# The softmax maximum of a stretch of context: an all-reduce on GpSimd in place of transposes and a product with a diagonal

## The chip, the cores and the metric

The kernel runs on one core of one Trainium2 chip. The metric is the device time of one execution, in microseconds (us). Engines are named as in the profile: PE (TensorE, PEld for its weight loads), DVE (VectorE), ACT (ScalarE), POOL (GpSimd), SP (SyncE, which issues the DMAs here).

## What is computed

One layer of a perceiver: cross attention between 256 latent tokens and a context of 25088 rows, then self attention, then a mixture of experts, everything in float32 with 512 features. The change lies in the cross attention, from latents to context:

```
h = layernorm(x)                                   # x: 256 x 512
Q = h @ Wq_c.T + bq_c;  K = ctx @ Wk_s.T + bk_s;  V = ctx @ Wv_s.T + bv_s
char2sub = softmax(Q @ K.T / sqrt(512)) @ V        # over 25088 context rows
sub2char = (context queries over the latents, interpolated back to 256)
gate = sigmoid(concat(char2sub, sub2char) @ Wg.T + bg)
x = x + gate * char2sub + (1 - gate) * sub2char
x = x + self_attention(layernorm(x))
x = x + shared_ffn(layernorm(x)) + routed_expert_ffn(layernorm(x))   # 32 experts, one per token
```

## The kernel before

The keys' weights are folded into the queries ahead of the loop (`aT`, and `cq` for the part that comes from the keys' bias), and the values' weights are applied behind it. In the loop a score is therefore `ctxT` times `aT`, and the output `o_sb` collects the probabilities times raw context rows. A score tile has context rows on its 128 partitions and the 256 latent tokens along its columns, so the softmax's maximum of a token is a maximum over partitions.

The context comes in 49 blocks of 512 rows. A stretch is three blocks (`SPAN`), so there are 16 full stretches and a last one of one block, 17 in all. For each stretch:

- `score` runs 48 matmuls of 128x256 (L392) into PSUM banks of the pool `ps_mm`, which has four. ACT copies each pair to `st` (L396), and DVE keeps a running maximum `mx` (L398, L400, L401). The columns' last maximum, L401, leaves one 128x256 tile.
- `maxima` turns `mx` into the running maximum per token, in two forms. As a column per token (`m_new`, tokens on partitions): two transposes on PE (L409) and a reduce on DVE (L411), `cq` added, maximum with the old one. `alpha` is the factor by which the old output shrinks. As a row of tokens on all partitions (`mbc`): `m_new` less `cq` scales an identity (`dg`, L428), a matmul with ones spreads it over partitions (L430), and ACT copies it out of PSUM (L432).
- `exponentials` subtracts `mbc` from each pair of `st` on DVE (L440), takes the exponential on ACT (L443) and adds the pairs up on POOL (L445, L447) into `ls`, then into `l_acc` with the factor `al` (L452 to L456).
- `width_sums` (`diffs`, L484 to L487) and `token_sums` (`sums`, L496 to L499) prepare on DVE the operands of `products`: a fast multiplication scheme with seven matmuls of 128x256 (L519) for each half block, 42 in a stretch.
- `collect` adds the four banks to `o_sb` on DVE. Its row `u2` shares one buffer (the tag "row", one buffer) with `dg` and `al`.

The program's order puts the stretches one inside the other: while PE runs `score(s + 1)`, DVE works on `token_sums(s)` and two blocks of `width_sums`. Then PE runs `products(s)`, while DVE, ACT and POOL do `maxima(s + 1)` and `exponentials(s + 1)`, and DVE the third block's `width_sums`. The framework schedules instructions on each engine within this order; each engine works its queue in order. Before the loop, scores and maxima of stretch 0 have no products beside them. Behind the loop, `weigh_last` handles the last block, and a matmul with ones sums `l_acc` over partitions (L572).

Of the kernel before, what the change touches and what calls it, by code (L numbers as in the profile page):

```python
# [2 lines left out]

# [7 lines left out]
F32 = mybir.dt.float32  # L11
I32 = mybir.dt.int32
AF = mybir.ActivationFunctionType
ALU = mybir.AluOpType
AX = mybir.AxisListType

P = 128
H = 512
KC = H // P
N = 256  # L20
NT = N // P
# [27 lines left out]
def perceiver_layer(  # L49
# [23 lines left out]
    nc = tc.nc  # L73
# [5 lines left out]
    small = ctx.enter_context(tc.tile_pool(name="small", bufs=4))  # L79
# [4 lines left out]
    def mm_bank(name):  # L84
        return ps_mm.tile([P, 512], F32, tag="mm", name=name)
# [4 lines left out]
    def tr_bank(name):  # L90
        return ps_tr.tile([P, 512], F32, tag="tr", name=name)
# [54 lines left out]
    ident = cpool.tile([P, P], F32, tag="ident", name="ident")  # L146
    make_identity(nc, ident)
    ones = cpool.tile([P, P], F32, tag="ones", name="ones")
# [107 lines left out]
    cq = first_half.tile([P, NT], F32, tag="cq", name="cq")  # L256

    with tc.tile_pool(name="pro", bufs=1) as pro:
# [18 lines left out]
        for t in range(NT):  # L277
            pm = mm_bank(f"cq_{t}")
            for c in range(KC):
                nc.tensor.matmul(  # L280
                    pm[:, 0:1], qT[:, c, ts(t, P)], bias_col("bk_s", c),
                    start=(c == 0), stop=(c == KC - 1),
# [22 lines left out]
        for n in (0, NT, 1, NT + 1):  # L305
            pm = mm_bank(f"s2_{n}")
            for c in range(KC):
                nc.tensor.matmul(
                    pm[:, :N], selT[:, c, ts(n, P)], bT[:, c, :],
                    start=(c == 0), stop=(c == KC - 1),  # L310
                )
            nc.vector.tensor_tensor(p2[:, n, :], pm[:, :N], bk, ALU.add)
            mx = small.tile([P, 1], F32, tag="s2_mx", name=f"s2_mx{n}")
# [17 lines left out]
        for t in range(NT):  # L331
            pm = mm_bank(f"vc_{t}")
            for c in range(KC):
                nc.tensor.matmul(
                    pm, xnT[:, c, ts(t, P)], wv_c_sb[:, c, :],
                    start=(c == 0), stop=(c == KC - 1),
                )
            evacuate(vc[:, t, :], pm)
        for k in range(NT):
            pt = tr_bank(f"p2T_{k}")  # L340
# [3 lines left out]
        for o in range(KC):  # L344
            pm = mm_bank(f"s2c_{o}")
            for k in range(NT):
                nc.tensor.matmul(
                    pm[:, :N], vc[:, k, ts(o, P)], p2T[:, k, :],
                    start=(k == 0), stop=(k == NT - 1),
# [27 lines left out]
    with tc.tile_pool(name="crows", bufs=3) as crows, tc.tile_pool(name="cwork", bufs=2) as cw:  # L377
        state = {"m": None, "mbc": None}

        def score(s):  # L380
            tiles = range(firsts[s], min(firsts[s] + SPAN, NBLK))
            n_pairs = 2 * len(tiles)
            st = cw.tile([P, 2 * SPAN, 2 * N], F32, tag="st", name=f"st_{s}")
            mx = cw.tile([P, 2 * N], F32, tag="rows", name=f"mx_{s}", bufs=1)
            for i in range(n_pairs):
                b, h = tiles[i // 2], i % 2
                if h == 0 and b + 2 < NBLK:
                    load_cols(b + 2)
                pm = mm_bank(f"sc_{s}_{i}")
                for u in range(2):  # L390
                    for c in range(KC):
                        nc.tensor.matmul(  # L392
                            pm[:, ts(u, N)], cols[b][:, c, ts(2 * h + u, P)], aT[:, c, :],
                            start=(c == 0), stop=(c == KC - 1),
                        )
                nc.scalar.copy(st[:, i, :], pm)  # L396
                if i == 1:
                    nc.vector.tensor_tensor(mx, st[:, 0, :], st[:, 1, :], ALU.max)  # L398
                elif i > 1:
                    nc.vector.tensor_tensor(mx, mx, st[:, i, :], ALU.max)  # L400
            nc.vector.tensor_tensor(mx[:, :N], mx[:, :N], mx[:, N:], ALU.max)  # L401
            return st, mx

        def maxima(s, mx):


            pt = mm_bank(f"mxT_{s}")
            for t in range(NT):
                nc.tensor.transpose(pt[:, ts(t, P)], mx[:, ts(t, P)], ident)  # L409
            m_new = small.tile([P, NT], F32, tag="m", name=f"m_{s}")  # L410
            nc.vector.tensor_reduce(  # L411
                m_new, pt[:, :N].rearrange("p (t q) -> p t q", t=NT), AX.X, ALU.max
            )
            nc.vector.tensor_tensor(m_new, m_new, cq, ALU.add)
            alpha = ones
            if s > 0:
                nc.vector.tensor_tensor(m_new, m_new, state["m"], ALU.max)
                dm = small.tile([P, NT], F32, tag="dm", name=f"dm_{s}")
                nc.vector.tensor_tensor(dm, state["m"], m_new, ALU.subtract)
                alpha = small.tile([P, NT], F32, tag="alpha", name=f"alpha_{s}")  # L420
                nc.scalar.activation(alpha, dm, AF.Exp, scale=xscale)
            state["m"] = m_new

            mc = small.tile([P, NT], F32, tag="mc", name=f"mc_{s}")
            nc.vector.tensor_tensor(mc, m_new, cq, ALU.subtract)
            dg = cw.tile([P, N], F32, tag="row", name=f"dg_{s}", bufs=1)
            for t in range(NT):
                nc.vector.tensor_scalar(dg[:, ts(t, P)], ident, mc[:, t : t + 1], None, ALU.mult)  # L428
            pb = mm_bank(f"mbc_{s}")
            nc.tensor.matmul(pb[:, :N], ones, dg, start=True, stop=True)  # L430
            mbc = cw.tile([P, 1, N], F32, tag="mbc", name=f"mbc_{s}")
            nc.scalar.copy(mbc[:, 0, :], pb[:, :N])  # L432
            return mbc, alpha

        def exponentials(s, st, mbc):
# [118 lines left out]
        nc.gpsimd.memset(o_sb, 0.0)  # L554
        st, mx = score(0)
        mbc, alpha = maxima(0, mx)
        exponentials(0, st, mbc)
        for b in range(3):
            load_rows(b)
        for s in range(len(firsts) - 1):  # L560
            st_next, mx = score(s + 1)
            a, sums = token_sums(s, st)
            ready = {b: width_sums(b) for b in range(firsts[s], firsts[s] + 2)}
            mbc, alpha_next = maxima(s + 1, mx)
            bank = products(s, a, sums, ready)
            exponentials(s + 1, st_next, mbc)
            collect(s, bank, alpha)
            st, alpha = st_next, alpha_next
# [10 lines left out]
    with tc.tile_pool(name="mix", bufs=1) as mp:  # L579
        oT = mp.tile([P, KC, N], F32, tag="oT", name="oT")  # L580
        for t in range(NT):
            pt = tr_bank(f"oT_{t}")
# [9 lines left out]
        for o in range(KC):  # L592
            for c in range(KC):
                nc.tensor.matmul(
                    gates[o][:, :N], wg_sb[:, KC + c, ts(o, P)], s2cT[:, c, :],
                    start=(c == 0), stop=False,
# [3 lines left out]
        for o in range(KC):  # L600
            pm = acc_bank(f"c2sT_{o}")
            for c in range(KC):
                nc.tensor.matmul(
                    pm[:, :N], wv_s_sb[:, c, ts(o, P)], oT[:, c, :],
                    start=(c == 0), stop=(c == KC - 1),
# [8 lines left out]
        for o in range(KC):  # L614
            pm = gates[o]
            for c in range(KC):
                nc.tensor.matmul(
                    pm[:, :N], wg_sb[:, c, ts(o, P)], c2sT[:, c, :],
                    start=False, stop=(c == KC - 1),
# [21 lines left out]
    with tc.tile_pool(name="att", bufs=1, reuse_waits="tile") as at:  # L641
        h1T = at.tile([P, KC, N], F32, tag="h1T", name="h1T")
        vh = at.tile([P, NT, HD], F32, tag="vh", name="vh")
        with tc.tile_pool(name="att1", bufs=1, reuse_waits="tile") as at1:
            h1 = at1.tile([P, NT, H], F32, tag="h1", name="h1")
            for t in range(NT):
                normalize(h1[:, t, :], x_sb[:, t, :], st1[:, t], f"ln1_{t}")
                pt = tr_bank(f"h1T_{t}")
# [139 lines left out]
    for t in range(NT):  # L788
# [3 lines left out]
        pt = tr_bank(f"h2T_{t}")  # L792
# [3 lines left out]
    mx = fp.tile([P, NT], F32, tag="mx", name="mx")  # L796
    for t in range(NT):
        pm = tr_bank(f"lg_{t}")
        for c in range(KC):
            nc.tensor.matmul(  # L800
                pm[:, :E], h2T[:, c, ts(t, P)], gw_sb[:, c, :],
                start=(c == 0), stop=(c == KC - 1),
# [318 lines left out]
```

## Time and profile before

| | us |
|---|---|
| median of three runs | 1304.01 (1302.05 to 1304.39) |
| profiled execution, its own time | 1304.49 |
| its span, first to last instruction | 1302.8 |
| PE busy, the whole span | 1161.5 (89%) |
| POOL busy, the whole span | 177.9 (14%) |
| cross attention over the context | about 60 to 723 |

Times in the profile count from the span's start. A row of the order of time gives start, length, engine, line, operation, output and inputs, and in square brackets how long the engine had been idle and what it waited for. A float32 matmul of 128x256 shows as two records. "L392" is line 392 of the kernel before; in the changed kernel, lines behind the change are five less. Behind the cross attention come self attention and the expert stage, whose chain is mostly DMA of expert weights.

### The profile page before, as it was taken

How to read it: one execution, taken by the hardware profiler on the slowest of the kernel's cores; microseconds unless marked ns; L12 is line 12 of the kernel's file. 1: busy time of each engine (PE TensorE's matmuls, PEld its weight loads, DVE VectorE, ACT ScalarE, POOL GpSimd, SP SyncE). 2: the span in 40 equal slices, each digit the busy share in tenths (PEclk: the TensorE clock that was granted, in tenths of full speed). 3: DMA queues.
4: the chain of work that ended last, by engine and by line, in shares of the span. 5: the costliest groups of instructions: out<-in, count | busy, mean ns of one | idle time of the engine just before them, and what ended most of it. 6: DMA issues, size and time to landing. Idle time of an engine off the chain costs nothing.

```text
span 1302.8 us, 16384 instructions
## 1 busy us (share of the span) xinstructions
PE 1161.5 (89%) x6796; PEld 842.8 (65%) x6796; DVE 617.4 (47%) x1079; ACT 227.3 (17%) x473; POOL 177.9 (14%) x149
## 2 busy tenths in 40 slices
PE   7989999999999999999999999898898677667665
PEld 6778888888888888888888656554544232222221
DVE  2257778877778777788776435511101010000000
ACT  0222212222212222122221223311000000000000
POOL 1023113332123331133322000000000000000000
PEclk9989999999999999999999999899999998988898
DMA  9544444444434454444431390599999999999995
GB/s 388 218 159 176 148 157 162 162 162 161 162 138 160 159 177 147 158 162 162 161 130 65 113 403 2 194 378 429 430 429 428 431 429 430 429 430 430 429 431 230
DMA packets 30892, 330.43 MB, mean 254 GB/s; under 512 B 3552, under 2 KB 3680, under 8 KB 4064
## 3 DMA queue, kind: packets, MB, share of 16 engines
q1 hardware_dynamic: 30816, 329.36, 63.6%
q8 instruction: 55, 0.90, 0.3%
q14 instruction: 21, 0.17, 0.0%
HBM read 328.82 MB, written 0.52 MB: 253 GB/s over the span
## 4 chain that ended last, share of the span: by engine, by line
PE 68%; DMA 27%; DVE 3%; issue 1%; ACT 1%; SPq 0%; DVEq 0%; ACTq 0%
PE sc L392 25%; PE p L519 21%; DMA rd<-in_ro_d_dram 9%; DMA rg<-in_ro_g_dram 9%; DMA ru<-in_ro_u_dram 8%; PE d L923 1%; PE ru L904 1%; PE rg L904 1%; PE acc L932 1%; PE y L750 1%; PE vh L659 1%; PE q L681 1%; PE k L681 1%; PE mbc L430 1%; PE shg L942 1%; PE qT L221 1%
## 5 line engine op out<-in xcount | busy, mean ns | idle before, releaser
L392 PE MATMUL sc<-aT,ctxT 128*128 128x256 f32 x1568 | 343.5, 381 | 0.6 <-DMA ctxT<-in_cxT_dram 0.6
L392 PEld LDWEIGHTS sc<-aT,ctxT 128*128 128x128 f32 x1568 | 299.4, 191 | 42.2 <-issue 1.0
L519 PE MATMUL p<-diffs,sums 128*128 128x256 f32 x576 | 155.8, 379 | 0.0
L519 PEld LDWEIGHTS p<-diffs,sums 128*128 128x128 f32 x576 | 109.4, 190 | 14.9
L923 PE MATMUL d<-rd,actT 128*32 128x512 f32 x512 | 75.5, 712 | 39.3 <-DMA rd<-in_ro_d_dram 31.0
L904 PE MATMUL ru<-ru,xg 128*32 128x256 f32 x1024 | 69.8, 415 | 41.4 <-DMA ru<-in_ro_u_dram 41.4
L396 ACT COPY st<-sc 128x512 f32<-128x512 f32 x98 | 57.4, 586 | 280.7 <-PE sc L392 280.7
L447 POOL TENSOR_TENSOR ls<-ls,st 128x512 f32<-128x512 f32 x64 | 97.1, 1517 | 33.8 <-ACT st L443 30.0
L400 DVE TENSOR_TENSOR mx<-mx,st 128x512 f32<-128x512 f32 x64 | 44.2, 691 | 116.1 <-ACT st L396 116.1
L519 PE MATMUL p<-ctx,st 128*128 128x256 f32 x384 | 98.5, 379 | 0.0
L930 DVE TENSOR_SCALAR selT<-keys,slot_key 128x256 f32<-128x256 f32 x32 | 11.2, 353 | 179.1 <-PE acc L932 179.1
L910 DVE TENSOR_TENSOR act<-act,ru 128x256 f32<-128x256 f32 x32 | 13.5, 422 | 167.8 <-PE ru L904 160.3
L445 POOL TENSOR_TENSOR ls<-st 128x512 f32<-128x512 f32 x17 | 25.1, 1476 | 493.8 <-ACT st L443 493.8
L904 PEld LDWEIGHTS ru<-ru,xg 128*32 128x32 f32 x1024 | 33.4, 119 | 75.1 <-DMA ru<-in_ro_u_dram 50.0
L932 PE MATMUL acc<-d,selT 128*128 128x512 f32 x128 | 66.3, 643 | 16.5 <-ACT d L101 16.5
L519 PEld LDWEIGHTS p<-ctx,st 128*128 128x128 f32 x384 | 72.9, 190 | 9.9
L443 ACT ACTIVATE st<-st 128x512 f32<-128x512 f32 x98 | 60.8, 630 | 100.2 <-DVE st L440 99.5
L440 DVE TENSOR_TENSOR st<-st,mbc 128x512 f32<-128x512 f32 x98 | 66.2, 718 | 21.8 <-ACT mbc L432 21.8
L484 DVE TENSOR_TENSOR diffs<-ctx 128x512 f32<-128x512 f32 x48 | 64.0, 1334 | 9.1 <-DMA ctx<-in_cx_dram 9.1
L904 PE MATMUL rg<-rg,xg 128*32 128x256 f32 x1024 | 63.9, 382 | 0.9 <-DVE xg L99 0.2
L923 PEld LDWEIGHTS d<-rd,actT 128*32 128x32 f32 x512 | 17.3, 120 | 68.8 <-issue 56.7
L932 PEld LDWEIGHTS acc<-d,selT 128*128 128x128 f32 x128 | 22.7, 198 | 59.9 <-ACT d L101 42.9
(235 smaller groups left out, 1321.4 us busy)
## 6 DMA issues: line engine op xcount, KB each, us to landing
rg<-in_ro_g_dram SPq DMA_DIRECT2D x32, 2048.0 KB, 37.9
ru<-in_ro_u_dram SPq DMA_DIRECT2D x32, 2048.0 KB, 38.9
rd<-in_ro_d_dram SPq DMA_DIRECT2D x32, 2048.0 KB, 38.9
ctxT<-in_cxT_dram SPq DMA_DIRECT2D x49, 1024.0 KB, 4.9
ctx<-in_cx_dram SPq DMA_DIRECT2D x49, 1024.0 KB, 4.9
sh<-in_sh_gu_dram SPq DMA_DIRECT2D x2, 2048.0 KB, 20.4
w_qc_ks<-in_w_qc_ks_dram SPq DMA_DIRECT2D x2, 1024.0 KB, 6.5
w_kc_qs<-in_w_kc_qs_dram SPq DMA_DIRECT2D x2, 1024.0 KB, 10.2
```

The costliest lines, as they stand in the source:

```text
L392: nc.tensor.matmul(pm[:, ts(u, N)], cols[b][:, c, ts(2 * h + u, P)], aT[:, c, :], start=(c == 0), stop=(c == KC - 1),)
L396: nc.scalar.copy(st[:, i, :], pm)
L400: nc.vector.tensor_tensor(mx, mx, st[:, i, :], ALU.max)
L440: nc.vector.tensor_tensor(pair, pair, mbc.to_broadcast([P, 2, N]), ALU.subtract)
L443: nc.scalar.activation(st[:, i, :], st[:, i, :], AF.Exp, scale=xscale)
L447: nc.gpsimd.tensor_tensor(ls, ls, st[:, i, :], ALU.add)
L484: nc.vector.tensor_tensor(t1, r[0][1], r[0][0], ALU.subtract)
L519: nc.tensor.matmul(bank[n][:, ts(o, half)], left[:, i, :], right[:, h, :], start=(i == 0 and o == 0), stop=(i == 2 * SPAN - 1 and (o == 1 ...
L681: nc.tensor.matmul(pm[:, :N], w[:, c, ts(hp, P)], h1T[:, c, :], start=(c == 0), stop=(c == KC - 1),)
L904: nc.tensor.matmul(pm[ts(q, CAP), : I // 4], xg[:, c, ts(j, CAP)], w[:, c, ts(q, I // 4)], start=(c == 0), stop=(c == KC - 1),)
L923: nc.tensor.matmul(pd[ts(q, CAP), :], actT[:, k, ts(q, CAP)], wd_e[:, 2 * q + k, :], start=(k == 0), stop=(k == 1),)
L932: nc.tensor.matmul(accs[t], slT[:, ts(t, P)], d, start=start, stop=stop)
```

## The change

`maxima` takes the other way round. POOL's `partition_all_reduce` makes the row form first: the maximum over all 128 partitions, on every partition, straight into `mbc`. DVE takes the maximum with the old `mbc`. The column form is picked from the diagonal: an elementwise product with the identity, summed along the columns, by `tensor_tensor_reduce`, once for each 128 tokens. `cq` is added, and `alpha` follows as before. The transposes, the diagonal, the product with ones and the copy out of PSUM are gone.

```diff
         def maxima(s, mx):
-            pt = mm_bank(f"mxT_{s}")
+            mbc = cw.tile([P, 1, N], F32, tag="mbc", name=f"mbc_{s}")
+            top = mbc[:, 0, :]
+            nc.gpsimd.partition_all_reduce(top, mx[:, :N], P, bass_isa.ReduceOp.max)
+            if s > 0:
+                nc.vector.tensor_tensor(top, top, state["mbc"][:, 0, :], ALU.max)
+
+            m_new = small.tile([P, NT], F32, tag="m", name=f"m_{s}")
+            at = cw.tile([P, N], F32, tag="row", name=f"at_{s}", bufs=1)
             for t in range(NT):
-                nc.tensor.transpose(pt[:, ts(t, P)], mx[:, ts(t, P)], ident)
-            m_new = small.tile([P, NT], F32, tag="m", name=f"m_{s}")
-            nc.vector.tensor_reduce(
-                m_new, pt[:, :N].rearrange("p (t q) -> p t q", t=NT), AX.X, ALU.max
-            )
+                nc.vector.tensor_tensor_reduce(
+                    at[:, ts(t, P)], top[:, ts(t, P)], ident, 1.0, 0.0, ALU.mult, ALU.add,
+                    accum_out=m_new[:, t : t + 1],
+                )
             nc.vector.tensor_tensor(m_new, m_new, cq, ALU.add)
             alpha = ones
             if s > 0:
-                nc.vector.tensor_tensor(m_new, m_new, state["m"], ALU.max)
                 dm = small.tile([P, NT], F32, tag="dm", name=f"dm_{s}")
                 nc.vector.tensor_tensor(dm, state["m"], m_new, ALU.subtract)
                 alpha = small.tile([P, NT], F32, tag="alpha", name=f"alpha_{s}")
                 nc.scalar.activation(alpha, dm, AF.Exp, scale=xscale)
             state["m"] = m_new
-
-            mc = small.tile([P, NT], F32, tag="mc", name=f"mc_{s}")
-            nc.vector.tensor_tensor(mc, m_new, cq, ALU.subtract)
-            dg = cw.tile([P, N], F32, tag="row", name=f"dg_{s}", bufs=1)
-            for t in range(NT):
-                nc.vector.tensor_scalar(dg[:, ts(t, P)], ident, mc[:, t : t + 1], None, ALU.mult)
-            pb = mm_bank(f"mbc_{s}")
-            nc.tensor.matmul(pb[:, :N], ones, dg, start=True, stop=True)
-            mbc = cw.tile([P, 1, N], F32, tag="mbc", name=f"mbc_{s}")
-            nc.scalar.copy(mbc[:, 0, :], pb[:, :N])
             return mbc, alpha
```

In the built program POOL's queue also gets two library reloads in each stretch, one ahead of the all-reduce and one ahead of the first addition behind it: the all-reduce and `tensor_tensor` are in different libraries of code. DVE's queue gets an instruction that reads the accumulator behind each `tensor_tensor_reduce`.

## The prediction

> **What bounds the kernel now.** I read the page first (busy shares, the chain that ended last), then the busy time by stretches, then the order of time within one stretch.
>
> The page's parts 1 and 4, and the busy time by stretches (us and instructions of PE, PEld, DVE, ACT, POOL; then granted clock, DMA share, GB/s):
>
> ```profile
> PE 1161.5 (89%) x6796; PEld 842.8 (65%) x6796; DVE 617.4 (47%) x1079; ACT 227.3 (17%) x473; POOL 177.9 (14%) x149
> ...
> PE sc L392 25%; PE p L519 21%; DMA rd<-in_ro_d_dram 9%; DMA rg<-in_ro_g_dram 9%; DMA ru<-in_ro_u_dram 8%; PE d L923 1%; PE ru L904 1%; PE rg L904 1%; PE acc L932 1%; PE y L750 1%; PE vh L659 1%; PE q L681 1%; PE k L681 1%; PE mbc L430 1%; PE shg L942 1%; PE qT L221 1%
> ...
> 330.00:370.00 40.00, 39.94 (x187) 34.78 (x186) 30.77 (x45) 8.55 (x16) 10.71 (x8) 1.00 0.45 160
> ```
>
> Scores (L392) and products (L519) hold 46% of the chain, and between 110 and 680 us PE is busy 39.94 us of 40 at full clock. So an instruction taken from PE there is worth its whole length, as long as nothing that PE waits for comes late. The later stage, where expert weights stream in, starts when this one ends, so what is saved here arrives at the end.
>
> The order of time in one stretch, around the maximum (start, length):
>
> ```profile
> 348.53 1.03 PE L519 MATMUL p<-ctx,st 128*128 128x256 f32 x4
> ...
> 350.08 0.42 DVE L401 TENSOR_TENSOR mx<-mx 128x256 f32<-128x256 f32 x1
> ...
> 350.69 0.38 PE L409 MATMUL mxT<-ident,mx 128*128 128x128 f32 x2
> ...
> 351.11 0.42 DVE L411 TENSOR_REDUCE m<-mxT 128x2 f32<-128x256 f32 x1 [0.61 <-PE mxT L409]
> ...
> 352.86 0.67 PE L430 MATMUL mbc<-dg,ones 128*128 128x256 f32 x2
> ...
> 353.97 2.50 DVE L440 TENSOR_TENSOR st<-st,mbc 128x512 f32<-128x512 f32 x4 [1.26 <-ACT mbc L432]
> ...
> 356.13 1.47 POOL L445 TENSOR_TENSOR ls<-st 128x512 f32<-128x512 f32 x1 [26.69 <-ACT st L443]
> ...
> 356.38 1.77 DVE L484 TENSOR_TENSOR diffs<-ctx 128x512 f32<-128x512 f32 x1
> ...
> 362.02 0.68 DVE L487 TENSOR_TENSOR diffs<-diffs,ctx 128x512 f32<-128x512 f32 x1
> ```
>
> Seen here: the chain from the ready mx (350.5) to the first subtraction (353.97) takes 3.5 us, while PE goes on with products. POOL had stood still for 26.69 us. A DVE operation of 0.68 us takes 1.77 when POOL's additions run beside it. And the third block's differences (L484 to L487) are ready at 362.70; the products that read them come next.
>
> **What leaves PE.** A stretch repeats every 39.79 us (the chain's score pieces start at 168.79, 208.59, 248.38). Its 96 score records take 20.72 us, 0.2158 each; 84 product records make 18.13 at that pace; together 38.85. The remaining 0.94 us are the transposes L409, the product L430 and their places in the queue. The change removes all three matmuls. There are 16 product phases with them in; the last is not paid, since there PE already waits 1.6 us for the sums of L499, a DVE wait that would only grow. 15 x 0.94 = 14.1 us.
>
> The first stretch is different: PE has no products then. It ends its scores at 82.05, waits 1.95 us for mx and 1.59 for dg, and starts the next scores at 86.99. In the changed order the next scores follow at once: 4.9 us. POOL may take some back: its five additions (1.47 each) and L449 (1.32) follow the first all-reduce, and the second one is wanted 20.7 us after the new start of scores plus 2, at 104.8. With two reloads (below) of R between, POOL is free at 94.8 + 2R: in time for R up to 5, 4.4 us late at R = 7.2. I take 3 us of the 4.9.
>
> ACT loses the copy L432 (0.37) and DVE the reduce, two small operations and dg; ACT and DVE wait for other engines around these places, so that is worth nothing by itself.
>
> **What comes in.** The changed program's queues show, in each stretch: on POOL a library reload, the all-reduce, another reload, then the additions. On DVE after L401: the maximum with the old mbc (waits for POOL), two tensor_tensor_reduce with an accumulator read each, six subtractions, the third block's first three differences, al, the fourth difference. So DVE stands still through the all-reduce, with all of this queued behind it, and PE waits for the fourth difference. That is the deadline.
>
> Let P0 be PE's first product (348.53). mx is ready at P0 + 2.0. The product that needs the fourth difference is the 34th: P0 + 33 x 0.4317 = 14.25, its weights 0.2 earlier: 14.05. Behind an all-reduce of length A, ending at P0 + 2.1 + A: hand-over and maximum 0.5 (a 128x256 DVE operation takes 0.42); the two reduces with reads 0.8 to 0.9 (no row shows the operation; half of a 128x256 operation is about 0.25, a 128x2 one 0.16); six subtractions at 0.607 and two small ones, 3.8; three differences at 0.6, al 0.35, the fourth 0.68, making 2.8; and one POOL addition beside them, 1.1 (1.77 against 0.68). Only one, since POOL's second instruction is now the product with al, which waits for al itself. Sum: P0 + 11.1 + A. PE stalls by A - 2.9 where that is positive, in 15 stretches.
>
> **The all-reduce, A.** No row shows one. Below: a two-input POOL pass over 128x256 with nothing beside it, 0.72 (shortest L455). Above: seven halving passes over 128 partitions at 1.05 each (median L455), 7.4. I take two passes, 2.1 us: one that folds the columns together, one that hands the result back; POOL is alone then, DVE waiting, so passes may be nearer 0.72. Then the fourth difference comes 0.8 us early and PE does not stall. Cover gone, each further microsecond costs 15.
>
> [...]
>
> **The reloads, R.** [...] Nearest rows: ACT_TABLE_LOAD 1.28 us, and the 26 KB bias transfer among others, 7.2 us. I take the middle, some 4 us. Both reloads have cover. The one before the all-reduce stands behind only POOL's own additions: 2.1 + 10.7 + 2R and a wait of a few us for al fill some 25 of 38.9 us at R = 4, 28 at 7.2; POOL becomes the bound only at about 13. The one behind it delays additions which nobody needs before the row buffer is written at the end of products (P0 + 18.1; al is read by P0 + 14), and and the last of them end some 4 us ahead of the matmul that sums l_acc, once the shift is counted.
>
> [...]
>
> **Sum.** 14.1 + 3 = 17.1 off the profiled execution's 1304.49 (span 1302.8 and 1.7 around it): 1287.4. The median of the runs is 0.5 lower, 1304.01, so 1287. This case's own range is 1283 (16 phases and all of the first 4.9) to 1301 (A near 3.9).
>
> **Rivals.**
> *The all-reduce is slower than two passes.* [...] It turns the sum at A = 4.0 (a stall of 1.1 eats 0.94 and the first stretch's 3). At 7.4: 15 x (4.5 - 0.94) = 53 us slower, 1357; the first stretch's gain is gone as well. Chance 0.18, a third of it for lengths beyond 7.4.
>
> *The reload is not hidden: the code arrives only when the all-reduce is called, after mx.* Then A + R stands on DVE's wait. R = 1.3: 3.4, stall 0.5, still faster; R = 4: 6.1, stall 3.2, 34 us slower, 1338; R = 7.2: 9.3, stall 6.4, 82 us slower, 1386. [...] Against: the reload is its own instruction in POOL's queue and has over 10 us there before mx is ready. [...] Chance 0.17.
>
> *Gain and stall cancel*, A at about 4 with all else as computed: 1304, chance 0.05.
>
> That the matmuls stay is excluded by the changed program, whose PE queue runs from products to scores without them.
>
> **How the numbers follow.** The forecast has 0.60 (faster, 1287), cancelling 0.05, the slower two together 0.35. A measurement of this kernel can tell 0.2% (2.6 us) from no change. Forecast and cancelling hold 0.65, so the range must reach into the rivals: up to 1386, the dear end of the second, which also holds the first up to its row bound. It leaves out the all-reduces beyond 7.4 us (0.06) and what the sums missed. Low end 1283.
>
> **What would show it.** PE's records per stretch fall from 187 in 40 us to products and scores alone, the period goes to 38.9 us, and PE's waits name no diffs or DVE at L514. The all-reduce's length A in POOL's rows, or better the time from L401's end to DVE's maximum, under 2.9 us. DVE's idle time before that maximum with POOL as releaser, 16 times about 2.2 us. POOL's gap between all-reduce and first addition is R. The forecast is wrong if PE waits for DVE's fourth difference in each stretch; the length of that wait times 15, less 17, is then the change.

## The result and the profile after

The changed kernel takes 1279.38 us in the median (1276.96 to 1282.87), the kernel before beside it 1304.2: a ratio of 0.9821, 95% interval 0.9804 to 0.9837, so 24.8 us less. The forecast was 17.1 us less. The direction and the mechanism of the steady loop held; the time lies below the range's low end of 1283.

The profiled execution after took 1276.96 us with a span of 1275.1, 27.7 below the span before. A further profile of the same kernel has a span of 1280.1, so single profiles of it differ by 5 us, and I count gains between fixed points inside one profile.

The page's parts 1, 4 and 5 of the kernel after, and the busy time of the same stretch of 40 us (columns: window, length, then PE, PEld, DVE, ACT, POOL busy, granted clock, DMA share, GB/s):

```profile
PE 1142.2 (90%) x6728; PEld 833.0 (65%) x6728; DVE 568.1 (45%) x1079; ACT 216.9 (17%) x456; POOL 197.9 (16%) x166
...
PE sc L392 26%; PE p L514 22%; DMA rd<-in_ro_d_dram 9%; DMA rg<-in_ro_g_dram 9%; DMA ru<-in_ro_u_dram 8%; PE ru L899 1%; PE rg L899 1%; PE d L918 1%; PE acc L927 1%; PE y L745 1%; PE vh L654 1%; PE q L676 1%; PE k L676 1%; PE shg L937 1%; PE shu L937 1%
...
L409 POOL PARTITION_ALL_REDUCE mbc<-mx x17 | 18.8, 1104 | 360.2 <-DVE mx L401 352.9
...
330.00:370.00 40.00, 40.00 (x187) 35.22 (x186) 27.61 (x44) 7.85 (x15) 11.55 (x9) 1.00 0.47 165
```

Scores and products (now L514) still carry the chain, PE is busy all 40.00 us, and the 17 all-reduces take 18.8 us of POOL in all. The 187 records in 40 us are as many as before, now all of scores and products, since more of a stretch fits in. The order of time around the maximum, kernel after:

```profile
335.31 1.03 PE L514 MATMUL p<-ctx,st 128*128 128x256 f32 x4
...
336.86 0.42 DVE L401 TENSOR_TENSOR mx<-mx 128x256 f32<-128x256 f32 x1
337.42 1.08 POOL L409 PARTITION_ALL_REDUCE mbc<-mx  x1 [19.54 <-DVE mx L401]
338.54 0.43 DVE L411 TENSOR_TENSOR mbc<-mbc,mbc 128x256 f32<-128x256 f32 x1 [1.26 <-POOL mbc L409]
339.00 0.29 DVE L416 CUSTOM_DVE_ANT_0 at<-mbc,ident 128x128 f32<-128x128 f32 x1
...
339.43 0.69 DVE L435 TENSOR_TENSOR st<-st,mbc 128x512 f32<-128x512 f32 x1
...
345.32 0.69 DVE L482 TENSOR_TENSOR diffs<-diffs,ctx 128x512 f32<-128x512 f32 x1
346.03 1.25 POOL L440 TENSOR_TENSOR ls<-st 128x512 f32<-128x512 f32 x1 [7.52 <-DVE diffs L482]
```

The all-reduce takes 1.08 us, DVE's wait for it 1.26, and the first subtraction starts 2.15 us behind the ready mx, against 3.5 before. POOL waited 19.54 us with the all-reduce at its head, and it starts 0.14 us behind mx: no time for its reload shows between the two. Its first addition starts 7.52 us behind the all-reduce. The profile puts this wait down to the difference that ended just before it (L482). In 14 of the 17 stretches it names nothing there (`issue`), for 6.7 to 7.3 us and once 8.95, and I read this as the other reload. The fourth difference (L482) is ready at 346.01, P0 + 10.7, and PE's product that needs it comes at P0 + 14.05.

All of PE's waits between 60 and 720 us (engine, line, what it waited for: total, times, longest), before and then after:

```profile
PE mxT L409 <- DVE mx L401: 2.0, 1, 2.0
PE p L519 <- DVE sums L499: 1.6, 1, 1.6
PE mbc L430 <- DVE dg L428: 1.6, 1, 1.6
PE sc L392 <- DMA ctxT<-in_cxT_dram: 0.6, 1, 0.6
```

```profile
PE p L514 <- DVE sums L494: 0.5, 1, 0.5
PE p L514 <- DVE diffs L482: 0.4, 1, 0.4
PE p L514 <- DVE diffs L480: 0.4, 1, 0.4
PE mix L622 <- DVE mixT L620: 0.2, 1, 0.2
```

No wait repeats from stretch to stretch. Where the time went, from the chain of waits of the two profiles (us from the span's start; each row begins where the one above it ends):

| | before | after | gain |
|---|---|---|---|
| first score of stretch 0 to first score of stretch 2 | 60.49 to 129.00 | 59.61 to 120.50 | 7.62 |
| to the first score of stretch 15 (13 periods) | 646.34 | 625.55 | 12.29 |
| to the matmul that sums l_acc | 713.80 | 690.00 | 3.01 |

That is 22.9 us. Another 0.9 lies ahead of the first score and 3.9 behind the loop, where both kernels run the same instructions; I don't credit these to the change. The further profile of the new kernel gives 62.63, 505.05 and 64.44 us between the same points, gains of 5.9, 12.3 and 3.0, 21.2 in all. In it PE waits 0.56 us for a DMA in the first block of scores, as it does before (0.61), and the second all-reduce starts 5.8 us behind its mx, against 4.9 in the profile shown. Behind the loop it has 588.7 us, where the profile shown has 585.1 and the one before 589.0, so the 3.9 there is scatter.

### The profile page after: what moved, and what is told of

Same layout as the page of the kernel before. It is cut to its first block, busy times and chain, and to the rows that moved or that the text cites. A ratio compares the mean times of both kernels' runs of the same rounds, so it can differ in the third digit from the quotient of the medians.

```text
span 1275.1 us, 16300 instructions
## 1 busy us (share of the span) xinstructions
PE 1142.2 (90%) x6728; PEld 833.0 (65%) x6728; DVE 568.1 (45%) x1079; ACT 216.9 (17%) x456; POOL 197.9 (16%) x166
## 4 chain that ended last, share of the span: by engine, by line
PE 69%; DMA 27%; DVE 3%; issue 1%; ACT 1%; POOL 0%; SPq 0%; DVEq 0%; ACTq 0%
PE sc L392 26%; PE p L514 22%; DMA rd<-in_ro_d_dram 9%; DMA rg<-in_ro_g_dram 9%; DMA ru<-in_ro_u_dram 8%; PE ru L899 1%; PE rg L899 1%; PE d L918 1%; PE acc L927 1%; PE y L745 1%; PE vh L654 1%; PE q L676 1%; PE k L676 1%; PE shg L937 1%; PE shu L937 1%
## 5 line engine op out<-in xcount | busy, mean ns | idle before, releaser
L514 PE MATMUL p<-diffs,sums 128*128 128x256 f32 x576 | 155.9, 379 | 0.4 <-DVE diffs L480 0.4
L514 PEld LDWEIGHTS p<-diffs,sums 128*128 128x128 f32 x576 | 109.4, 190 | 15.6 <-DVE diffs L480 0.8
L442 POOL TENSOR_TENSOR ls<-ls,st 128x512 f32<-128x512 f32 x64 | 104.1, 1627 | 3.8
L400 DVE TENSOR_TENSOR mx<-mx,st 128x512 f32<-128x512 f32 x64 | 47.0, 735 | 123.0 <-ACT st L396 122.6
L899 PE MATMUL ru<-ru,xg 128*32 128x256 f32 x1024 | 66.2, 398 | 37.3 <-DMA ru<-in_ro_u_dram 37.3
L514 PE MATMUL p<-ctx,st 128*128 128x256 f32 x384 | 98.5, 379 | 0.0
L925 DVE TENSOR_SCALAR selT<-keys,slot_key 128x256 f32<-128x256 f32 x32 | 11.2, 353 | 185.7 <-PE acc L927 185.7
L514 PEld LDWEIGHTS p<-ctx,st 128*128 128x128 f32 x384 | 73.0, 190 | 9.9
L409 POOL PARTITION_ALL_REDUCE mbc<-mx x17 | 18.8, 1104 | 360.2 <-DVE mx L401 352.9
L435 DVE TENSOR_TENSOR st<-st,mbc 128x512 f32<-128x512 f32 x98 | 62.7, 689 | 0.0
L899 PEld LDWEIGHTS rg<-rg,xg 128*32 128x32 f32 x1024 | 30.9, 111 | 41.9 <-issue 18.5
```

The costliest lines, as they stand in the source:

```text
L435: nc.vector.tensor_tensor(pair, pair, mbc.to_broadcast([P, 2, N]), ALU.subtract)
L442: nc.gpsimd.tensor_tensor(ls, ls, st[:, i, :], ALU.add)
L514: nc.tensor.matmul(bank[n][:, ts(o, half)], left[:, i, :], right[:, h, :], start=(i == 0 and o == 0), stop=(i == 2 * SPAN - 1 and (o == 1 ...
L899: nc.tensor.matmul(pm[ts(q, CAP), : I // 4], xg[:, c, ts(j, CAP)], w[:, c, ts(q, I // 4)], start=(c == 0), stop=(c == KC - 1),)
```

## Experiments

**The new kernel again.** No edit.

> The changed kernel once more, as the anchor for the others of this group. Both theories: about 25 us under the kernel before (ratio near 0.981).

Measured: 1278.97 us against 1303.51, ratio 0.9812 (0.9798 to 0.9827). The gain repeats on another occasion, 24.5 us.

**The first stretch alone, both ways.** One kernel is the new one with the old way in stretch 0, the other the old one with the all-reduce in stretch 0 only.

```diff
+            return (maxima_old if s == 0 else maxima_new)(s, mx)     # e1
+            return (maxima_old if s > 0 else maxima_new)(s, mx)      # e2
```

> The changed kernel with the old way (transposes, diagonal, product) for stretch 0 only. Theory 1, that 8 to 9 of the 25 us come from stretch 0 alone, where PE no longer stands between two blocks of scores and keeps its clock: 16 to 17 us under the kernel before (ratio 0.987 to 0.988), the second block of scores again about 22.5 us long, and the second all-reduce no longer late. Theory 2, that the surplus over the forecast comes from DVE and ACT being freer in every stretch: 20 us or more under it (0.985 or less).

> The kernel before with the all-reduce for stretch 0 only. Theory 1: 8 to 9 us under the kernel before (ratio 0.993 to 0.994); this and the run with the old way in stretch 0 add up to the whole gain. Theory 2: no more than the 4.9 us of PE's gap, ratio 0.996 or more.

Measured: 1286.95, ratio 0.9874 (0.9859 to 0.9889), 16.5 us less than before; and 1294.81, ratio 0.9939 (0.9925 to 0.9952), 8.7 us less. The two sum to 25.2, the whole change to 24.5. So the first stretch is worth about 8 us and not 3, and the parts add up. From first score to stretch 2 the second kernel takes 61.30 us (61.02 to 122.32) against 68.51: 7.2 less, with nothing but the first maximum changed. The gap of PE accounts for 5.1. The rest is in the next block of scores. PE's two waits in the kernel before, and the blocks of scores of stretches 1 and 2 from its chain of waits (start, length):

```profile
84.01 0.41 PE L409 MATMUL mxT<-ident,mx 128*128 128x128 f32 x2 [1.95 <-DVE mx L401]
86.00 1.19 PE L430 MATMUL mbc<-dg,ones 128*128 128x256 f32 x2 [1.59 <-DVE dg L428]
```

```profile
87.19 22.73 PE sc L392 x96
...
129.00 20.72 PE sc L392 x96
```

Windows of the kernel before, then of the kernel after:

```profile
82.10:87.10 5.00, 1.50 (x5) 1.14 (x6) 2.35 (x7) 0.58 (x1) 0.00 (x0) 0.72 0.57 210
87.20:91.20 4.00, 4.00 (x11) 3.12 (x11) 3.56 (x5) 2.84 (x5) 1.46 (x1) 0.51 0.01 4
91.20:95.20 4.00, 4.00 (x20) 3.54 (x19) 3.24 (x3) 1.85 (x3) 3.77 (x4) 1.00 0.00 0
```

```profile
82.10:87.10 5.00, 5.00 (x25) 4.39 (x24) 3.57 (x12) 2.33 (x5) 1.08 (x1) 1.00 0.46 184
87.20:91.20 4.00, 4.00 (x21) 3.51 (x20) 3.24 (x5) 2.23 (x5) 0.49 (x1) 1.00 0.73 238
```

Before, PE came out of its gap at half clock (granted clock 0.51) and ran 11 records in 4 us where it runs 20 or 21 at full clock (1.00); the block of 96 records took 22.73 us in place of 20.72. These 2.0 us are invisible as a wait: PE counts as busy. The kernel with the old way in stretch 0 alone has the long block again, 22.90 us. The next two kernels try this reading. Some 4 us at 0.51 stand behind two waits of 1.95 and 1.59 us, with 0.41 us of matmuls between. In the run with three all-reduces below, half clock came in the last phase after 2.6 us of waiting.

**The gap kept, but filled.** The kernel before, with matmuls into an unused bank placed in PE's two waits of stretch 0 (four ahead of the transposes, three ahead of the product with the diagonal).

```diff
+            if s == 0:
+                fill = tr_bank("fill_a")
+                for k in range(4):
+                    nc.tensor.matmul(fill[:, :N], aT[:, 0, :P], aT[:, k, :], start=(k == 0), stop=(k == 3))
             pt = mm_bank(f"mxT_{s}")
             for t in range(NT):
                 nc.tensor.transpose(pt[:, ts(t, P)], mx[:, ts(t, P)], ident)
+            if s == 0:
+                fill = tr_bank("fill_b")
+                for k in range(3):
+                    nc.tensor.matmul(fill[:, :N], ident, mx[:, :N], start=(k == 0), stop=(k == 2))
```

> The kernel before with seven matmuls of no use put on PE around stretch 0's maximum, so that PE's gaps are filled and nothing else changes. If the 2 us by which the next block of scores runs longer (22.7 against 20.7) are a clock taken away after an idle PE: that block takes 20.7 us again, granted clock 1.00 in it, and the time is 1 to 2.5 us under the kernel before. If the block is long for another reason (late ctxT, copies on ACT): still 22 to 23 us, and the time is the same or a little above.

Measured: 1299.51, ratio 0.9981 (0.997 to 0.9991), 3.0 us less, a little more than the 1 to 2.5 expected. More work and less time: the next block of scores takes 20.72 us again, as the windows of this kernel show:

```profile
82.00:86.40 4.40, 3.45 (x16) 2.47 (x16) 2.35 (x7) 0.40 (x1) 0.00 (x0) 1.00 0.67 238
86.40:90.40 4.00, 4.00 (x20) 3.51 (x20) 3.56 (x5) 2.84 (x5) 1.46 (x1) 1.00 0.02 4
```

**The gap filled with useful work, without any all-reduce.** The kernel before, with the first maximum and its exponentials moved between two pairs of the next block's scores.

```diff
                 nc.scalar.copy(st[:, i, :], pm)
+                if i == 0 and between is not None:
+                    between()                  # maxima(0), exponentials(0)
...
+            st_next, mx = score(s + 1, of_first if s == 0 else None)
```

> The kernel before, old way throughout, but the maximum of stretch 0 is taken behind the first pair of the next scores, so PE has work in the gap; no all-reduce anywhere. If the gain of stretch 0 is one of PE's order and not of the all-reduce: PE's wait before the next scores goes from 3.5 to about 1.5 us, the scores run at full clock, 5 to 7 us under the kernel before (ratio 0.995 to 0.996). If only the all-reduce brings it: no change.

Measured: 1297.73, ratio 0.9961 (0.9949 to 0.9973), 4.8 us less. One wait of 1.6 us for dg is left, and the scores behind it run at full clock (80 records in 17.27 us, granted clock 1.00 from 84 to 100 us). From the first score to stretch 2 it takes 63.40 us, 5.1 less than before, where the all-reduce in stretch 0 alone gave 7.2. So most of the first stretch's gain belongs to the order of the first two stretches, and could be had without GpSimd. The wait that is left is most of the 2.1 by which it stays short.

**The first stretch's additions on DVE.** The new kernel, with the additions of stretch 0 taken from POOL, so that no reload stands between its first two all-reduces.

```diff
+        def adder(s):
+            return nc.vector if s == 0 else nc.gpsimd
...
-                    nc.gpsimd.tensor_tensor(ls, st[:, 0, :], st[:, 1, :], ALU.add)
+                    adder(s).tensor_tensor(ls, st[:, 0, :], st[:, 1, :], ALU.add)
...
```

> The changed kernel with the additions of stretch 0 on DVE, so that POOL runs no reload between the first and the second all-reduce. If the second all-reduce comes late because of the two reloads (7.2 us each in the trace), it now starts within 0.3 us of its mx, PE waits for no diffs in the first products, and the time is about 1 us (0.1%) under that of the changed kernel. If the lateness were DVE's own, the stalls stay.

Measured: 1280.58, ratio 0.9826 (0.9812 to 0.9839), not faster than the new kernel beside it (1278.97). The mechanism is there, its size is below what the times tell. In the kernel after, POOL is late for the second all-reduce, and PE's products of stretch 0 wait twice:

```profile
90.71 1.37 POOL L440 TENSOR_TENSOR ls<-st 128x512 f32<-128x512 f32 x1 [7.18 <-issue]
...
99.39 1.05 POOL L444 TENSOR_TENSOR l_acc<-ls 128x256 f32<-128x256 f32 x1
107.71 1.08 POOL L409 PARTITION_ALL_REDUCE mbc<-mx  x1 [7.27 <-issue]
...
114.81 1.13 PE L514 MATMUL p<-diffs,sums 128*128 128x256 f32 x4 [0.38 <-DVE diffs L480]
...
116.35 0.70 PE L514 MATMUL p<-diffs,st 128*128 128x256 f32 x2 [0.41 <-DVE diffs L482]
```

The mx of stretch 1 was ready at 102.85 and the all-reduce started 4.86 us later; in between POOL had stood idle for 7.18 and 7.27 us with nothing named as releaser, which I read as the two reloads. PE lost 1.3 us by it: this product phase takes 19.44 us, the edited kernel's 18.13, with no wait for diffs. In the further profile of the new kernel the same phase takes 20.39, so there the lateness costs 2.3.

**Longer all-reduces.** The new kernel with three and with six all-reduces in a chain; the maximum stays the same.

```diff
-            nc.gpsimd.partition_all_reduce(top, mx[:, :N], P, bass_isa.ReduceOp.max)
+            for k in range(2):                                       # 5 for six
+                nc.gpsimd.partition_all_reduce(
+                    mx[:, ts((k + 1) % 2, N)], mx[:, ts(k % 2, N)], P, bass_isa.ReduceOp.max
+                )
+            nc.gpsimd.partition_all_reduce(top, mx[:, ts(0, N)], P, bass_isa.ReduceOp.max)   # ts(1, N) for six
```

> The changed kernel with three all-reduces one behind the other in each stretch (the maximum of the maximum), A about 3.4 us in place of 1.1. The trace of the changed kernel has the fourth difference ready 3.4 us before PE asks for it, so nothing is lost in stretches 2 to 15; the prediction's formula, A - 2.9, would lose 0.5 us in each, 8 us. In stretch 1, where POOL is already late, both lose about 4 us. So 3 to 5 us over the changed kernel by the trace, about 12 by the formula.

> Six all-reduces in each stretch, A about 6.7 us. The scheduler puts the third block's differences behind three subtractions here, not six. The prediction's formula as it stands gives a stall of 3.8 in each of 15 stretches, 57 us, and 10 more in stretch 1. With the order of this kernel, the fourth difference is ready about 14.8 us behind PE's first product, wanted at 14.05: 0.8 in each, 12 us, and 10 in stretch 1. So 15 to 25 us over the changed kernel by the order, 65 by the formula.

Measured: 1289.49, ratio 0.9897 (0.9875 to 0.9919), and 1312.03, ratio 1.0071 (1.0048 to 1.0095); some 10.5 and 33 us above the new kernel. PE's waits of the first, then of the second:

```profile
PE p L518 <- DVE diffs L484: 3.7, 1, 3.7
PE p L518 <- DVE sums L498: 1.8, 1, 1.8
```

```profile
PE p L518 <- DVE diffs L484: 10.1, 1, 10.1
PE p L518 <- DVE diffs L486: 8.3, 14, 0.6
```

With three, DVE waits 3.6 us for POOL in a stretch of the middle, and the period is still 38.85 us. The forecast's formula, which turns at 2.9, has 0.7 us of stall per stretch there, some 10 us in all. The total of 10.5 meets that by chance: all of it lies at the loop's two ends (6.1 us up to stretch 2, 5.4 behind the start of the last full product phase), where waits of 3.7 and 1.8 us are followed by records at half clock (granted clock 0.64 from 119.4 to 127.4 us, 0.50 from 684 to 688). With six, DVE waits 7.05 us and PE 0.6 us in each of 14 stretches; the period is 39.71, so the loop costs 11.2 and its ends 20.7. The scheduler moved the third block's differences ahead of three subtractions in that kernel, so the chain that the forecast had fixed gives way. The turning point exists, between 3.6 and 7.05 us, and the sizes expected missed in both directions.

**The reload put behind the ready mx.** A multiplication of one column by ones stands on POOL ahead of the all-reduce. It waits for mx, and in the built program the reload stands between it and the all-reduce.

```diff
+            nc.gpsimd.tensor_tensor(mx[:, 0:1], mx[:, 0:1], ones[:, 0:1], ALU.mult)
             nc.gpsimd.partition_all_reduce(top, mx[:, :N], P, bass_isa.ReduceOp.max)
```

> The changed kernel with a multiplication of one column of mx by one on POOL ahead of each all-reduce, which waits for mx; the reload now stands behind mx, not ahead of it, so A + R = about 8.6 us lie on the chain. This is the second rival of the prediction, made on purpose; its formula gives a stall of 5.7 in each of 15 stretches, some 70 us over the changed kernel with the 0.9 kept. But the scheduler has moved the third block's differences ahead of DVE's wait here; then PE waits for nothing in the middle stretches, and only stretch 1 and the first exponentials lose: 5 to 15 us over the changed kernel.

Measured: 1285.55, ratio 0.9875 (0.9853 to 0.9896), some 6.5 us above the new kernel's 1278.97 (7.8 by the distances from the kernels before beside them). The all-reduce starts 6.3 us behind the multiplication (idle 106.7 over 17), and yet the loop loses nothing: stretch 15 starts at 625.32 (625.55 in the new kernel), because the third block's differences were scheduled ahead of DVE's wait. The price is at the end, where nothing is left to cover it: in the last product phase PE waits 0.86 and 1.88 us for DVE, and then 3.15 us for l_acc. In this kernel's order of time:

```profile
676.92 0.57 POOL L409 TENSOR_TENSOR mx<-mx,ones 128x1 f32<-128x1 f32 x1 [3.90 <-DVE mx L401]
683.23 1.08 POOL L410 PARTITION_ALL_REDUCE mbc<-mx  x1 [5.74 <-issue]
...
692.00 1.25 POOL L441 TENSOR_TENSOR ls<-st 128x512 f32<-128x512 f32 x1 [7.69 <-issue]
...
695.61 0.70 PE L568 MATMUL l<-l_acc,ones 128*128 128x256 f32 x2 [3.15 <-POOL l_acc L452]
```

This also shows what the changed kernel does not do: there, the reload is not paid behind mx. The forecast's rival of 34 to 82 us would not have come true even with it paid there.

**All additions on DVE.** The same `adder`, returning DVE for every stretch, so that no addition stands between POOL's all-reduces.

> The changed kernel with all of POOL's additions on DVE: POOL runs all-reduces alone, with one reload in all. DVE takes 8 operations more in a stretch (about 4.7 us) and is slowed by POOL no more (about 5 us less). [...] If DVE's queue gets too long for the fourth difference, PE waits in each stretch and the time rises by 5 us or more.

Measured: 1285.31, ratio 0.9876 (0.9854 to 0.9897), some 6 us above the new kernel. The loop is not the cause: from stretch 2 to stretch 15 it takes 505.05 us in both, and PE's products wait for nothing. The cause stands at the start. The first score comes at 64.69 us in place of 59.61. POOL shows a single long gap without a releaser in this kernel, 11.10 us. It lies ahead of POOL's mask for the identity, which PE's first transposes read. The built program has a reload at that place, as that of the kernel before has, where no gap shows; I read the gap as this reload, and why it is long here was not shown (this kernel's order of time):

```profile
12.24 0.28 POOL masks.py:199 TENSOR_SCALAR_AFFINE_SELECT ident<-ident 128x128 f32<-128x128 f32 x1 [11.10 <-issue]
...
12.57 0.69 PE L211 MATMUL xnT<-ident,xn 128*128 128x128 f32 x2 [12.57 <-POOL ident masks.py:199]
```

In the new kernel PE starts that line at 7.06. So the 6 us say nothing of DVE's queue; with additions on POOL or on DVE the loop took the same time.

**The last product phases.** Behind stretch 15's scores come one full product phase, a third of a block of scores and the last product phase. One kernel is the new one with the old way in the last stretch's maximum (e10), one the old one with the new way there alone (e11), and one the new one with the old way in the maximum just ahead of it (e12).

```diff
+            return (maxima_old if s == len(firsts) - 1 else maxima_new)(s, mx)   # e10
+            return (maxima_old if s < len(firsts) - 1 else maxima_new)(s, mx)    # e11
+            return (maxima_old if s == len(firsts) - 2 else maxima_new)(s, mx)   # e12
```

> The new kernel with the old way (transposes, diagonal product) for the last stretch's maximum alone. Theory 1 (the last product phase gains twice: three matmuls leave PE, 0.94 us, and the shorter chain from mx to the first subtraction brings the last sums 1.15 us earlier): 2.1 us over the new kernel, PE's wait for the sums in the last phase back at 1.6 us from 0.5, the phase's products 20.9 us long from 18.85. Rival (the forecast's step: the last phase is bound by the sums and gains nothing): the same as the new kernel. Second rival (only the matmuls count): 0.9 over it, with PE's wait for the sums at 0.5.

> The kernel before with the all-reduce for the last stretch's maximum alone. Theory 1: 2.1 us below the kernel before, PE's wait for the sums in the last phase down from 1.6 to 0.5 us, no other wait of PE changed. Rival (the forecast's step): no change, or slower by the reload of POOL's library, which here is paid once behind 38 us of POOL's other work.

> The new kernel with the old way for the last stretch but one alone: its maximum lies in the product phase ahead of the last. Theory 1, mended (in that phase the old way keeps DVE's queue late, by the longer chain to the first subtraction and by the additions of POOL beside the differences; DVE's chain of sums then starts late, which only the last phase feels): 2.1 us over the new kernel, 0.94 of it the three matmuls, PE's wait for the sums in the last phase back at 1.6 us from 0.5. Rival (only the matmuls count wherever they stand; the wait was shortened by something else, such as the moved start of the whole loop): 0.9 over it, the wait at 0.5.

| kernel | median, ratio | these phases, start to the gate's first matmul | PE's wait for the last sums |
|---|---|---|---|
| before | | 667.06 to 714.39: 47.33 | 1.6 |
| new way in the last alone (e11) | 1300.88, 0.9984 (0.9972 to 0.9995) | 667.44 to 713.84: 46.40 | 1.6 |
| old way in the one ahead (e12) | 1283.28, 0.9851 (0.983 to 0.9872) | 647.32 to 693.72: 46.40 | 1.6 |
| old way in the last (e10) | 1281.91, 0.9845 (0.983 to 0.986) | 648.19 to 693.44: 45.25 | 0.5 |
| after | | 646.27 to 690.59: 44.32 | 0.5 |

My Theory 1 for the first two of these fell: the last maximum is worth 0.93 us both ways, its matmuls alone, and the wait for the sums doesn't move with it. In its mended form it held: the maximum just ahead is worth 2.08 us in the profile, 0.93 for its matmuls and 1.15 in the last phase's wait. The times, against the new kernel's 1279 of another occasion, say 3 and 4 us; the interval of e12 (1280.8 to 1286.2) holds the profile's 1281, that of e10 (1281.1 to 1285.0) ends just above its 1280. How a maximum reaches into the next phase is seen on DVE. The kernel before, in the product phase that starts at 667.06, then the kernel after, in the one that starts at 646.27:

```profile
672.34 2.50 DVE L440 TENSOR_TENSOR st<-st,mbc 128x512 f32<-128x512 f32 x4 [1.26 <-ACT mbc L432]
674.75 1.76 DVE L484 TENSOR_TENSOR diffs<-ctx 128x512 f32<-128x512 f32 x1
...
688.08 0.95 DVE L496 TENSOR_TENSOR sums<-st 128x768 f32<-128x768 f32 x1
```

```profile
653.98 0.69 DVE L479 TENSOR_TENSOR diffs<-ctx 128x512 f32<-128x512 f32 x1
...
664.51 1.63 DVE L491 TENSOR_TENSOR sums<-st 128x768 f32<-128x768 f32 x1 [0.31 <-PE p L514]
```

Before, DVE's queue runs without a break into the sums and reaches them 21.0 us behind the phase's start, its differences taking 1.76 us beside POOL's additions. After, these differences take 0.69, since POOL's additions start only at 656.25, 6.95 us behind the all-reduce, and the sums start at 18.2, as soon as PE has released the buffer. In the loop 20.7 us of scores stand between, and PE waits for the sums in neither kernel; only the last phase, with a third of them, shows the difference.

## Why the prediction was right, and where it was wrong

**The periodic term is right.** 15 x 0.94 = 14.1 was forecast. The period fell from 39.79 to 38.85, and 13 of them gave 12.29 us; with the phases at either end, whose three matmuls also left, 14.2.

**The first stretch failed, by the term "I take 3 of 4.9".** Apart from its 0.94 it gave 6.7 us in the profile shown and 4.9 in the further one; by the times with the change there alone or left out there, 8 to 9. The gap was 5.1. Not seen was the half clock behind it, 2.0 us, although the profile of before had it: its second block of scores takes 22.73 us where the later ones take 20.72, and the window there grants less than full clock (0.51 from 87.2 to 91.2 us). The 1.9 us that I took back for the late second all-reduce were 1.3, and 2.3 in the further profile. The first block of scores took 0.8 longer in the profile of before, for a DMA; the further profile of the new kernel has that wait too, so it is no gain of the change. POOL's two gaps of 7.2 us did make that all-reduce late, by 4.86 us where 4.4 were worked out. That 1.9 came near is luck: R was taken too short, and the slack behind the all-reduce too small, 0.8 us for 3.4 (below). The low end of the range was also added up wrongly: 16 phases and 4.9 off 1304 are 1284 and not 1283.

**The last phase failed, by the step "a DVE wait that would only grow".** It gave 2.1 us where 0 was forecast. The matmuls stand behind that wait in PE's queue, so their 0.93 us are paid in any case; and the wait shrank by 1.15, since DVE comes out of the phase ahead of it earlier. I had looked at what the change adds to DVE there, and not at what it takes from DVE's queue one phase earlier.

**A was too long, R too short, and neither moved the sum in the loop.** A is 1.085 us (1.082 to 1.410) where I took 2.1 between 0.72 and 7.4; R, read from POOL's gaps, is about 7.2 where I took 4. The fourth difference came at P0 + 10.7, while P0 + 11.1 + A gives 12.2: the POOL addition of 1.1 that I put beside it starts later, 7.52 us behind the all-reduce. So the slack was 3.4 us and not 0.8.

**The rivals.** The slower all-reduce is excluded by its 1.085 us. The unhidden reload is excluded by the 0.14 us between mx and the all-reduce. Gain and stall did not cancel either: in the steady loop PE waits for no difference. The point from which either decides lies higher than 2.9 us, as the runs with three and six showed, since the slack was 3.4 us, and a longer wait leads to another schedule.

**The sum.** 14.17 + 6.68 + 2.07 = 22.92 between fixed points, against 17.1; the further profile has 21.2. What is left of the medians' 24.5 and 24.8, some 2 to 4 us, I can't place. The part behind the loop alone differs by as much between two profiles of the new kernel (585.1 and 588.7).

## What to carry to other kernels

The bubble on PE cost its length here, 5.1 us, and 2.0 us more at half clock (0.51) behind it in which PE looks busy: compare the length of equal blocks of matmuls behind each bubble before pricing its removal. Seven spare matmuls in the bubble won the second part alone (the block took 20.72 us again, from 22.73). When an engine's instruction waits in a steady loop, price its effect also in the last turn, where the cover is shorter, and one turn ahead of the wait, where the queue that ends in it begins. For an operation that no row shows, a turning point worked out with a fixed order of the other queues is a lower bound as long as a scheduler may reorder them.

## What the runs showed of the hardware

- `partition_all_reduce` with a maximum over 128 partitions and 256 float32 columns took 1.085 us on POOL (median of 17); in the chain of six one followed another in 1.16 us.
- Between this operation and `tensor_tensor` POOL stood idle for some 7 us, mostly with "issue" as the end of the gap: 6.3 to the all-reduce in the late-reload kernel (mean of 17; 7.27 once in the new kernel), 6.7 to 7.3 back, once 8.95. At the start of the kernel with all additions on DVE, a gap was 11.10. Where the all-reduce had waited 19.54 us for mx, it started 0.14 us behind mx, with no such gap.
- Half clock (0.50 from 684 to 688 us) came on in the last product phase of the run with three all-reduces after waits of 0.75 and 1.81 us with 1.1 us of matmuls between, 2.6 us of waiting in all; a single wait of 1.6 us left the clock at 1.00 (the hoisted kernel, and the last phase of the kernel before). No half clock shows behind 0.86 and 1.88 us in the last phase of the late-reload kernel, 2.7 us in all and 1.1 us of matmuls between: the pairs of product records behind them took 0.59 us, where they took 1.06 in the run with three all-reduces. The length of the waits alone does not decide it, and no run here shows what does.
